# More loads spread over 14 of the 16 DMA engines, earlier field groups, and twelve differences moved to VectorE, in a bilinear pair kernel

## The chip, the cores and the metric

The kernel runs on one core of one Trainium2 chip. The metric is the device time of one execution in microseconds (us). The kernel before has a median of 753.25 us over four runs (753.73, 753.89, 752.77 and 752.07).

## The reference

There are 1024 samples with 32 fields of 128 numbers each, and one 128 x 128 matrix for each of the 496 pairs of fields. For each pair (i, j) the vector of field i is multiplied by the pair's matrix, and the result is multiplied, number by number, by the vector of field j.

```python
v_i = inputs[:, I_IDX, :]          # (1024, 496, 128)
v_j = inputs[:, J_IDX, :]
transformed = jnp.einsum('bpd,ped->bpe', v_i, W)
return transformed * v_j
```

All of it is float32. The output has 1024 x 496 x 128 numbers, 260 MB; the inputs have 49 MB together.

## The kernel before

The host lays the inputs out anew. `xt` holds each field with its 128 numbers down the partitions and the 1024 samples along a row. `wt` holds the matrices in chunks of eight (`WL`), one chunk of 512 KB per load. The pairs are taken with i from 30 down to 0, so that the first pairs need few fields, and the output leaves in groups of four pairs (`OG`), 2 MB each.

**One pair.** A pair is two halves of 512 samples; the loop variable `u` counts halves and `q` counts pairs. After the first 15 pairs, which are multiplied directly (L208), each half is three matrix products into one PSUM bank. The weights and the field are each split into a high part, a low part and a difference: `wh`, `wl`, `wd` (L127 to L130, for two pairs at once) and `xh`, `xl`, `xd` (L142 to L148, per half field). `first(u)` issues two of the products (L211) and lets ScalarE scale the bank (L212). `second(u)`, three halves later, issues the third (L220), and VectorE multiplies the bank by field j into the output tile `ot` (L226). ScalarE's queue issues the store of a finished tile (L257).

**Who splits.** ScalarE makes the high parts. GpSimd makes the low parts and the differences, with one exception: for the first fields that are split (i above 32 - 2 - `NATIVE` - `SHARED`, which is 15) the difference `xd` is put on a list called `later`, and VectorE makes it some halves afterwards (L264). For fields 15 to 0 GpSimd makes it (L148).

**Order.** The order of the program is written out by hand (`tc.manual_schedule()`): each engine and each queue works through its own instructions in the order in which the loop over `u` issues them, and waits where a buffer or an operand is not ready. The weight chunk `c` is loaded at the pair that `w_at` gives it, 17 pairs before its first pair for most of them, into one of three buffers.

**Output buffers.** The tiles of the output rotate over `s0`, `s1`, `s2` and, as long as they are free, over the four buffers `g0` to `g3`. Buffer `g{k}` is later filled with the fields 4k+1 to 4k+4 by one load of 2 MB (`load_group(k)`), at the pair `group_at` names; output tiles leave it alone from 20 pairs (`OWAIT`) before that. So there are seven buffers for output at first, and three from pair 293 on. In the kernel before, `g3`, `g2`, `g1`, `g0` are filled at pairs 79, 141, 219 and 313.

**Which DMA engines a load uses.** SyncE's queue spreads the 128 partitions of a load over 16 DMA engines, eight rows each. Seven of the weight chunks (`WAPART`) are loaded by `load_apart` in two parts instead. GpSimd's queue loads the first 112 partitions with 14 in the outermost place (L102), which makes 14 engines carry eight rows each; SyncE's queue loads the other 16 partitions (L103), one row to each of 16 engines. Some pairs later `move_on` issues a tiny load into a tile called `mark` (L99) that takes the two engines left out, so that the next load of this kind begins at the same engine again. The host puts the rows of these chunks into the order that this needs.

Of the kernel before, what the change touches and what calls it, by code (L numbers as in the profile page):

```python
# [11 lines left out]
P = 128  # L12
NF = 32
NQ = NF * (NF - 1) // 2
BT = 1024
# [3 lines left out]
OG = 4  # L19
EPS = 2.0**-12  # L20
NATIVE = 5
SHARED = 10
XDLAG = 10
LAG = 3
WB = 3
# [4 lines left out]
XG = 4  # L30
NE = 14
ROWS = 8 * NE
WAPART = (45, 47, 49, 51, 54, 58, 60)
BACK = 3
XWAIT = 12
OWAIT = 20
SLAG = 2

# [7 lines left out]
def kernel(  # L46
# [22 lines left out]
    nc = tc.nc  # L69
# [12 lines left out]
    def load_x(f, pieces=1, eng=None):  # L82
        if f == 0:

            t = rpool.tile([P, WL, P], F32, tag="w", name="x_0").rearrange("p q e -> p (q e)")
        else:
            t = xpool.tile([P, BT], F32, tag=f"x{f}", name=f"x_{f}")
        s = BT // pieces
        for k in range(pieces):
            (eng or nc.sync).dma_start(out=t[:, k * s : (k + 1) * s], in_=xt[f, :, k * s : (k + 1) * s])  # L90
        x_sb[f] = t
# [5 lines left out]
    def move_on(k):  # L97

        nc.gpsimd.dma_start(out=mark[: 2 * k], in_=xt[0, : 2 * k, :16].rearrange("(b a) n -> a b n", a=k))  # L99

    def load_apart(dst, src):
        nc.gpsimd.dma_start(out=dst[:ROWS], in_=src[:ROWS].rearrange("(b a) m n -> a b m n", a=NE))  # L102
        nc.sync.dma_start(out=dst[ROWS:], in_=src[ROWS:])  # L103

    def load_group(k):
        t = xpool.tile([P, XG, BT], F32, tag=f"g{k}", name=f"x_g{k}")
        f = XG * k + 1
        nc.sync.dma_start(out=t, in_=xt[f : f + XG].rearrange("m d b -> (m d b)").rearrange("(d m b) -> d m b", m=XG, b=BT))
        for m in range(XG):
            x_sb[f + m] = t[:, m, :]  # L110

    def load_w(c, splits=(0, WL), eng=nc.sync):
        w_raw[c] = rpool.tile([P, WL, P], F32, tag="w", name=f"w_{c}")
        if c in WAPART:
            load_apart(w_raw[c], wt[c])
            return
        for a, b in zip(splits, splits[1:]):
            eng.dma_start(out=w_raw[c][:, a:b, :], in_=wt[c, :, a:b, :])
# [17 lines left out]
    def split_x(f, a, u):  # L136
# [7 lines left out]
        nc.gpsimd.tensor_scalar(l, l.bitcast(F32), 1.0 / EPS, 1.0, ALU.mult, ALU.mult)  # L144
        if f > NF - 2 - NATIVE - SHARED:
            later.append((min(u + XDLAG, 2 * first_q[f] + LAG - 1), d, h.bitcast(F32), l.bitcast(F32)))
# [5 lines left out]
    first_q = {i: q for q, (i, j) in reversed(list(enumerate(pairs)))}  # L152
# [31 lines left out]
    back = []  # L184

    ngroup = NF // XG // 2
    group_at = {first_q[XG * k + XG + 1] - XWAIT: k for k in range(ngroup)}
    until = {f"g{k}": q - OWAIT for q, k in group_at.items()}
    used = {t: n - 9 for n, t in enumerate(("s0", "s1", "s2", *sorted(until, reverse=True)))}

# [10 lines left out]
    def first(u):  # L201
        q, h = divmod(u, 2)
        i, c = pairs[q][0], q // WC
        r = slice(q % WC * P, (q % WC + 1) * P)
        s = slice(h * HB, (h + 1) * HB)
        po[u] = ppool.tile([P, HB], F32, tag="po", name=f"po_{u}")
        if q < nq0:
            nc.tensor.matmul(po[u], w_raw[q // WL][:, q % WL, :], x_sb[i][:, s], start=True, stop=True)  # L208
        else:
            for t in (0, 1):  # L210
                nc.tensor.matmul(po[u], w_s[c][t][:, r], x_s[i][t][:, s], start=t == 0, stop=t == 1)  # L211
            nc.scalar.mul(po[u], po[u], 1.0 + EPS)  # L212

    def second(u):
        q, h = divmod(u, 2)
        i, j = pairs[q]
        r = slice(q % WC * P, (q % WC + 1) * P)
        s = slice(h * HB, (h + 1) * HB)
        if q >= nq0:
            nc.tensor.matmul(  # L220
                po[u], w_s[q // WC][2][:, r], x_s[i][2][:, s], start=False, stop=True, skip_group_check=True
            )
        g, k = divmod(q, OG)
        if k == 0 and h == 0:
            ots[g] = out_tile(g)
        nc.vector.tensor_tensor(ots[g][:, k, s], po.pop(u), x_sb[j][:, s], ALU.mult)  # L226
        if q >= NQ - 2:
            stores.append((u + SLAG, out[g, :, k, s], ots[g][:, k, s]))
        elif g == 0 or q >= NQ - OG:
            if h == 1:  # L230
                stores.append((u + SLAG, out[g, :, k], ots[g][:, k]))
        elif k == OG - 1 and h == 1:
            stores.append((u + SLAG, out[g], ots[g]))

    for u in range(2 * NQ + LAG + SLAG):
        q = u // 2
        if u < 2 * NQ:
            i, j = pairs[q]
            if u % 2 == 0 and j == i + 1 and XG * ngroup < i - 2 - XLEAD:
                load_x(i - 2 - XLEAD)  # L240
            first(u)
            if u == 2 * nq0:
                move_on(5)
            if u % 2 == 0 and q in group_at:
                load_group(group_at[q])
            if u % 2 == 1 and q in w_at:
                load_w(w_at[q])
                if w_at[q] in WAPART:
                    back.append(q + BACK)
            if u % 2 == 0 and q in back:  # L250
                move_on(16 - NE if q < w_q[WAPART[-1]] else 13)
            if u == 2 * x_at + 1:
                load_x(0)
        if LAG <= u < 2 * NQ + LAG:
            second(u - LAG)
        while stores and stores[0][0] <= u - LAG:
            nc.scalar.dma_start(*stores.pop(0)[1:])  # L257
        if u % 2 == 1:
            ready = [t for t in todo if t[0] <= q]
            if ready:  # L260
                ready[0][2](u)
                todo.remove(ready[0])
        while later and later[0][0] <= u:
            nc.vector.tensor_tensor(*later.pop(0)[1:], ALU.subtract)  # L264
# [33 lines left out]
```

## Time and profile before

| | before |
|---|---|
| median of four runs | 753.25 us |
| the profiled execution | 753.73 us |
| its span, first to last instruction | 752.0 us |
| TensorE (PE) busy | 701.1 us, 93% |
| VectorE (DVE) busy | 651.8 us, 87% |
| ScalarE (ACT) busy | 626.9 us, 83% |
| GpSimd (POOL) busy | 602.7 us, 80% |
| moved by DMA | 310.05 MB, 412 GB/s |
| queue q10 (ScalarE's issues: nearly all stores) | 261.10 MB, 82.2% of 16 engines' span |
| queue q1 (SyncE's issues: loads) | 45.03 MB, 15.4% |
| queue q0 (GpSimd's issues) | 3.22 MB, 1.2% |

An engine's busy time is the time in which one of its instructions runs. A DMA queue's share is the time that its packets took, over sixteen engines for the whole span. A queue name with a q at its end (SPq, ACTq, POOLq) is the part of an engine that issues transfers. Times in the profile count from the first instruction.

### The profile page before, as it was taken

The page shows a single profiled execution, that of the slowest core. Times are in us where ns is not written, and L with a number is a line of the kernel's source. Part 1 is how long each engine was busy: PE and PEld are TensorE (multiplying, and loading weights), DVE is VectorE, ACT ScalarE, POOL GpSimd, SP SyncE. Part 2 cuts the span into 40 slices and gives each one's busy share as a digit, 9 for nine tenths or more (in the row PEclk, how much of TensorE's full clock was granted, in tenths as well). Part 3 has the DMA queues.
Part 4 walks back from the last instruction along what each step waited for, and adds up shares of the span by engine and source line. Part 5 has one row for each costly group of instructions (what it writes and reads, how often), then busy time and mean ns, then how long its engine had stood idle before and what let it go on. Part 6 is the DMA issues. An engine that isn't in the chain of part 4 may idle for free.

```text
span 752.0 us, 10964 instructions
## 1 busy us (share of the span) xinstructions
PE 701.1 (93%) x2946; PEld 552.4 (73%) x2946; DVE 651.8 (87%) x1012; ACT 626.9 (83%) x1256; POOL 602.7 (80%) x878
## 2 busy tenths in 40 slices
PE   7998999999999999989999997899999999999993
PEld 3576777777778778767777776678778787777782
DVE  4899999998999999777889877789898989788893
ACT  1298889998889889878898895789999898888892
POOL 1789999999999898886988875878888979797670
PEclk9999999999999999999999998999999999999997
DMA  9999999999999999999999997999999999999997
GB/s 344 422 430 428 410 427 392 423 431 428 430 412 429 430 424 428 424 421 424 414 428 408 418 411 302 374 429 427 417 418 429 413 425 409 427 426 423 420 417 300
DMA packets 31790, 310.05 MB, mean 412 GB/s; under 512 B 3953, under 2 KB 4081, under 8 KB 15601
## 3 DMA queue, kind: packets, MB, share of 16 engines
q10 hardware_dynamic: 19584, 261.10, 82.2%
q1 hardware_dynamic: 10880, 45.03, 15.4%
q0 software_dynamic: 1264, 3.22, 1.2%
q8 instruction: 24, 0.39, 0.2%
q14 instruction: 38, 0.30, 0.1%
HBM read 49.29 MB, written 260.05 MB: 411 GB/s over the span
## 4 chain that ended last, share of the span: by engine, by line
PE 61%; DMA 19%; POOL 9%; DVE 6%; issue 2%; ACT 1%; DVEq 0%; ACTq 0%; POOLq 0%
PE po L211 39%; PE po L220 19%; DMA out_dram<-ot 19%; DVE ot L226 5%; PE po L208 4%; POOL xd L148 3%; POOL wl L128 2%; POOL xl L143 2%; POOL xl L144 1%; POOL wd L130 1%; DMA x<-in_xt_dram 1%; POOL wd L129 1%; DVE xd L264 1%; ACT po L212 0%; ACT wh L127 0%
## 5 line engine op out<-in xcount | busy, mean ns | idle before, releaser
L212 ACT ACTIVATE po<-po 128x512 f32<-128x512 f32 x962 | 545.7, 583 | 92.8 <-PE po L211 49.3
L226 DVE TENSOR_TENSOR ot<-po,x 128x512 f32<-128x512 f32 x720 | 464.1, 685 | 68.2 <-DMA out_dram<-ot 33.9
L211 PE MATMUL po<-xl,wl 128*128 128x512 f32 x962 | 378.8, 394 | 17.7 <-POOL wl L128 16.4
L211 PE MATMUL po<-xh,wh 128*128 128x512 f32 x962 | 379.3, 394 | 14.8 <-DVE ot L226 14.5
L220 PE MATMUL po<-xd,wd 128*128 128x512 f32 x962 | 376.2, 391 | 1.8 <-DVE xd L264 0.9
L128 POOL TENSOR_TENSOR wl<-w,wh 128x256 fp32r<-128x256 f32 x241 | 181.0, 751 | 66.7 <-ACT wh L127 64.4
L211 PEld LDWEIGHTS po<-xh,wh 128*128 128x128 f32 x962 | 181.5, 189 | 62.9 <-DVE ot L226 24.7
L211 PEld LDWEIGHTS po<-xl,wl 128*128 128x128 f32 x962 | 181.4, 189 | 62.7 <-POOL wl L128 24.5
L220 PEld LDWEIGHTS po<-xd,wd 128*128 128x128 f32 x962 | 181.6, 189 | 40.8 <-ACT po L212 2.4
L130 POOL TENSOR_TENSOR wd<-wl,wd 128x256 fp32r<-128x256 f32 x241 | 178.1, 739 | 20.1
L226 DVE TENSOR_TENSOR ot<-po,x_g 128x512 f32<-128x512 f32 x272 | 172.2, 684 | 21.0 <-DMA out_dram<-ot 10.0
L129 POOL TENSOR_SCALAR wd<-wh 128x256 fp32r<-128x256 f32 x241 | 98.6, 409 | 20.4
L127 ACT ACTIVATE wh<-w 128x256 fp32r<-128x256 f32 x241 | 99.3, 412 | 5.2 <-DVE ot L226 5.2
L148 POOL TENSOR_TENSOR xd<-xh,xl 128x512 fp32r<-128x512 f32 x32 | 41.4, 1292 | 2.7
L143 POOL TENSOR_TENSOR xl<-x_g,xh 128x512 fp32r<-128x512 f32 x32 | 41.5, 1296 | 0.2 <-ACT xh L142 0.2
L143 POOL TENSOR_TENSOR xl<-x,xh 128x512 fp32r<-128x512 f32 x20 | 26.3, 1315 | 15.7 <-ACT xh L142 15.4
L144 POOL TENSOR_SCALAR xl<-xl 128x512 fp32r<-128x512 f32 x52 | 34.8, 670 | 4.6
L208 PE MATMUL po<-x,w 128*128 128x512 f32 x60 | 29.0, 644 | 4.1 <-DMA x<-in_xt_dram 4.1
L208 PEld LDWEIGHTS po<-x,w 128*128 128x128 f32 x60 | 11.9, 205 | 20.4 <-issue 12.3
L142 ACT ACTIVATE xh<-x 128x512 fp32r<-128x512 f32 x20 | 12.4, 628 | 11.4 <-DMA x<-in_xt_dram 11.3
L142 ACT ACTIVATE xh<-x_g 128x512 fp32r<-128x512 f32 x32 | 20.2, 631 | 0.0
L264 DVE TENSOR_TENSOR xd<-xh,xl 128x512 fp32r<-128x512 f32 x20 | 19.8, 989 | 0.0
(7 smaller groups left out, 11.2 us busy)
## 6 DMA issues: line engine op xcount, KB each, us to landing
out_dram<-ot ACTq DMA_DIRECT2D x122, 2048.0 KB, 13.9
w<-in_wt_dram SPq DMA_DIRECT2D x54, 512.0 KB, 10.8
x_g<-in_xt_dram SPq DMA_DIRECT2D x4, 2048.0 KB, 18.9
x<-in_xt_dram SPq DMA_DIRECT2D x14, 512.0 KB, 9.5
w<-in_wt_dram POOLq DMA_DIRECT2D x7, 448.0 KB, 12.2
out_dram<-ot ACTq DMA_DIRECT2D x6, 512.0 KB, 9.4
x<-in_xt_dram ACTq DMA_DIRECT2D x4, 256.0 KB, 5.9
out_dram<-ot ACTq DMA_DIRECT2D x4, 256.0 KB, 8.3
```

The source lines that it names most:

```text
L127: nc.scalar.mul(h, raw, 1.0 - 2.0**-13)
L128: nc.gpsimd.tensor_tensor(l, raw, h.bitcast(F32), ALU.subtract)
L129: nc.gpsimd.tensor_scalar(d, h.bitcast(F32), EPS, 1.0, ALU.mult, ALU.mult)
L130: nc.gpsimd.tensor_tensor(d, l.bitcast(F32), d.bitcast(F32), ALU.subtract)
L143: nc.gpsimd.tensor_tensor(l, x_sb[f][:, s], h.bitcast(F32), ALU.subtract)
L144: nc.gpsimd.tensor_scalar(l, l.bitcast(F32), 1.0 / EPS, 1.0, ALU.mult, ALU.mult)
L148: nc.gpsimd.tensor_tensor(d, h.bitcast(F32), l.bitcast(F32), ALU.subtract)
L208: nc.tensor.matmul(po[u], w_raw[q // WL][:, q % WL, :], x_sb[i][:, s], start=True, stop=True)
L211: nc.tensor.matmul(po[u], w_s[c][t][:, r], x_s[i][t][:, s], start=t == 0, stop=t == 1)
L212: nc.scalar.mul(po[u], po[u], 1.0 + EPS)
L220: nc.tensor.matmul(po[u], w_s[q // WC][2][:, r], x_s[i][2][:, s], start=False, stop=True, skip_group_check=True)
L226: nc.vector.tensor_tensor(ots[g][:, k, s], po.pop(u), x_sb[j][:, s], ALU.mult)
```

## The change

Three numbers and the rules around them change.

- `load_group` sends groups 1 and 2 (fields 5 to 8 and 9 to 12) through `load_apart`, as eight more weight chunks now are. These are chunks 20, 26, 30, 32, 36, 38, 40 and 42, all before the seven that were there. Each such load is followed by a `move_on`.
- The groups are loaded at pairs 52, 129, 207 and 313, given in a list; `until`, which says how long a group's buffer serves for output, follows from it.
- `SHARED` goes from 10 to 16, so VectorE also makes the differences of fields 15 to 10, two halves each.

```diff
-SHARED = 10
+SHARED = 16
...
-WAPART = (45, 47, 49, 51, 54, 58, 60)
+WAPART = (20, 26, 30, 32, 36, 38, 40, 42, 45, 47, 49, 51, 54, 58, 60)
 BACK = 3
-XWAIT = 12
+XAT = (313, 207, 129, 52)
+XAPART = (1, 2)
...
-        nc.sync.dma_start(out=t, in_=xt[f : f + XG].rearrange("m d b -> (m d b)").rearrange("(d m b) -> d m b", m=XG, b=BT))
+        rows = xt[f : f + XG].rearrange("m d b -> (m d b)").rearrange("(d m b) -> d m b", m=XG, b=BT)
+        if k in XAPART:
+            load_apart(t, rows)
+        else:
+            nc.sync.dma_start(out=t, in_=rows)
...
-    group_at = {first_q[XG * k + XG + 1] - XWAIT: k for k in range(ngroup)}
+    group_at = {q: k for k, q in enumerate(XAT)}
+    assert all(q < first_q[XG * k + XG + 1] for q, k in group_at.items())
...
                 load_group(group_at[q])
+                if group_at[q] in XAPART:
+                    back.append(q + BACK)
...
-    for f in range(1, XG * 4, XG):
-        xt[f : f + XG] = xt[f : f + XG].transpose(1, 0, 2).copy().reshape(XG, P, BT)
+    for k in range(4):
+        f = XG * k + 1
+        some = xt[f : f + XG].transpose(1, 0, 2).copy()
+        if k in XAPART:
+            some[:ROWS] = some[:ROWS].reshape(NE, 8, XG, BT).transpose(1, 0, 2, 3).reshape(ROWS, XG, BT).copy()
+        xt[f : f + XG] = some.reshape(XG, P, BT)
```

## The prediction

> **What bounds the kernel now.** I read the page's slices first, then busy time by stretch, then the waits in the stretch that stands out, then the packet records of the trace (queue, start, duration and size of every DMA packet).
>
> ```profile
> span 752.0 us, 10964 instructions
> DMA  9999999999999999999999997999999999999997
> GB/s 344 422 430 428 410 427 392 423 431 428 430 412 429 430 424 428 424 421 424 414 428 408 418 411 302 374 429 427 417 418 429 413 425 409 427 426 423 420 417 300
> ```
>
> The DMA engines are busy all the time, while PE has 93%, DVE 87%. So bytes per engine set the time. One place in mid-span is open: slices 25 and 26, about 451 to 489 us, with 302 and 374 GB/s. Busy time by stretch (start:end, length, busy by engine, then granted PE clock, DMA share, GB/s):
>
> ```profile
> core 0: us, PE busy (x) PEld busy (x) DVE busy (x) ACT busy (x) POOL busy (x), PEclk, DMA share, GB/s
> 200.00:330.00 130.00, 123.32 (x536) 100.02 (x537) 117.42 (x176) 115.57 (x234) 114.90 (x166) 1.00 1.01 424
> 330.00:448.00 118.00, 112.62 (x476) 89.16 (x475) 98.03 (x160) 102.43 (x205) 95.43 (x142) 0.99 1.00 417
> 448.00:484.00 36.00, 29.53 (x119) 23.60 (x119) 26.86 (x40) 25.59 (x52) 24.50 (x36) 0.91 0.82 336
> 457.00:459.00 2.00, 2.00 (x6) 1.56 (x5) 1.97 (x4) 1.02 (x2) 0.00 (x0) 0.50 0.19 80
> 484.00:600.00 116.00, 111.59 (x484) 89.97 (x483) 100.49 (x161) 103.56 (x209) 97.95 (x147) 1.00 1.01 422
> ```
>
> At 457 us most DMA engines are empty and PE runs at half its clock. The waits of 440 to 484 us say what came before:
>
> ```profile
> DVE ot L226 <- DMA out_dram<-ot: 7.8, 2, 6.9
> PEld po L211 <- DVE ot L226: 5.8, 1, 5.8
> ```
>
> DVE stood 6.9 us until a store had left its buffer (448 to 454.9 us); PE stood behind it, came back at clock 0.5, and fed the stores too slowly.
>
> Why was that store late when the engines are empty just after? Its sixteen end markers (4-byte packets) tell. It was issued at 437.2 us; eleven engines ended it by 445.2 us, the last one at 454.2. One engine was 9 us behind. The packets say why: from 165 to 310 us, where chains of packets can be followed engine by engine, 16 KB usually lasts 611 ns on fifteen engines and 635 on one, 4 KB 159 against 166. One engine is 4% slow. Its lag behind the middle one grows from nothing at 30 us to 2.9 at 165, near 4 at 205 and 7.7 at 306; a lag of 9 us with three or four buffers is the stall.
>
> Store latency (issue to landing) agrees. The first line is 330 to 448 us, the second 484 to 600, where chunks 45 to 54 already go over 14 engines:
>
> ```profile
> out_dram<-ot ACTq DMA_DIRECT2D x19, 2048.0 KB, 17.6
> out_dram<-ot ACTq DMA_DIRECT2D x21, 2048.0 KB, 11.5
> ```
>
> In that later part the lag stays near 2 us, so the slow engine must be one of the two left out; the packet durations of those loads fit too.
>
> **The change part by part.** The sum is against the profiled run (753.73 us, span 752.0); its median is 0.5 us less.
>
> *Relief of the slow engine.* A chunk load gives it 1 row of 4 KB instead of 8, the other fourteen 9: relative to them 8 x 159 ns = 1.27 us. A group load does it with 16 KB rows: 8 x 611 ns = 4.9 us. The lag grows 3.5 us per 100 us (4.8 in 140). Group 2 at about 204 us takes the 4 us away; from there to 317 us come 4.0, chunks 20, 26 take 2.5; group 1 takes the rest; from 317 to 480 us come 5.7, chunks 30 to 40 take 6.4. So around 450 us the lag should be 0 to 2 us, and the 6.9 us stall has no cause. What is late next is the middle engine, at 8 us after issue against three buffers' 16 us.
>
> *What the hole is worth.* 36 us x (1 - 336/422) = 7.3 us. In 330 to 448 us the slow engine set the pace while the others ran thin: 118 x (1 - 417/424) = 1.9 us. After 484 us the relieving loads are unchanged, so the 3 us by which the slow engine ends last (750.3 against 747.4) remain; I take 0.5 us, between 0 and 3.
>
> *What it costs.* The other fourteen engines carry one more row per load: 2 x 611 + 8 x 159 ns = 2.5 us, in full, since they will set the pace.
>
> *GpSimd.*
>
> ```profile
> L102 POOL DMA_DIRECT2D w<-in_wt_dram x7: 622/622/625, 523.1 to 693.6; - x7
> L99 POOL DMA_DIRECT2D mark<-in_xt_dram x8: 632/633/746, 31.4 to 699.0; - x8
> L148 POOL TENSOR_TENSOR xd<-xh,xl x32: 1263/1296/1304, 170.6 to 663.5; 128x512 fp32r<-128x512 f32 x32
> L264 DVE TENSOR_TENSOR xd<-xh,xl x20: 682/868/1573, 19.1 to 157.7; 128x512 fp32r<-128x512 f32 x20
> ```
>
> Ten loads and ten `mark` issues more: 10 x (0.62 + 0.63) = 12.6 us; twelve differences fewer: 12 x 1.30 = 15.5. Net 3 us less: nothing. A 2 MB issue by GpSimd is in no row; with as many rows as a chunk, 0.62 us is the near value; if each row were cut into four, 2.5 us, once per group. In its queue the weight splits wait behind it, and PE behind those. It must not meet a wait there: group 2's buffer last holds output group 22, landed at 163.6 us in this trace, and GpSimd reaches the load at about 204 (start of chunk 67's split); group 1: group 43, 289.4 against 312. SyncE's 16-row parts wait on the same buffers: no wait.
>
> *VectorE.* Twelve differences at 0.87 to 0.99 us: 10.4 to 11.9 us between about 180 and 330 us. By busy time this fills it: 117.4 of 130 us already. But its operations overlap: six in a row took 3.69 us, 0.615 us each, against PE's 0.45 + 0.23 = 0.68 per half (two L211 and one L220 in the chain). For the 100 pairs from 120 to 219, 200 x 0.615 + 11.9 = 135 us against PE's 136 and the DMA engines' 25 groups x 5.8 = 145 (5.8 us between store issues from 338 to 448 us). Cost 0; without the overlap 200 x 0.685 + 11.9 = 149, 4 us over DMA (bound 0 to 12).
>
> *Earlier groups.* Group 3's buffer is last used by output group 3 (landed 49.5 us), so SyncE can issue the load at about 78 us (now 112.7); weight loads behind it wait only the issue, 0.5 us. Up to 35 us earlier, 5 us of DMA time moves and none is added. Output has six buffers instead of seven for some 45 us, and latency there is 10.5 us against six buffers' 33: 0, between -1 and +1. Groups 2 and 1 were issued at 205.6 and 317.9 and move a few us; each is needed some 30 us later.
>
> Sum: -7.3 - 1.9 - 0.5 + 2.5 = -7.2, so 746.5 for such an execution and 746.0 for a median.
>
> *A rule against it.* All loads on 16 engines in 330 to 448 us left one engine 9 us behind the rest. The Trainium skill, "DMA: Bandwidth & Descriptors", section "Rules for kernel authors", says to use all 16 engines and put a multiple of 16 outermost, which treats them as equal; by it the sum would be +2.5 us alone. The same page ("Latency and other measured facts") calls two engines usually slower and guesses at the software queue's descriptor rings; by that guess ten more GpSimd loads would feed the slowness. This trace speaks against the guess: the 4% was measured where no such load runs.
>
> **The rivals.**
>
> *VectorE becomes the bound (slower).* For it: 97% busy (67.95 of 70 us) from 130 to 200 us. Against it: the 0.615 us pitch. It decides once a half costs VectorE over 0.68 us with the differences in: 200 x 0.685 + 11.9 is 13 us over PE; if the whole 12.7 us reaches the stores, -7.2 + 12.7 = +5.5, about 758.5. Stores in flight (15 to 19 us of latency) would hide most of it. Chance 0.09.
>
> *The hole stays.* Three buffers start at pair 293 and group 0's 2 MB still go over 16 engines by SyncE. If another stall of over 3 us halves the clock there, only 1.9 + 0.5 - 2.5 is left: 753. Chance 0.09.
>
> *The relief does not reach the slow engine* (the 14 engines begin elsewhere): +2.5, 755.5; the flat lag after 484 us speaks against it. Chance 0.03.
>
> *More is gained.* The slow engine's 3 us at the end go too, and 90 to 120 us, where stores were briefly slower, gains 2: 741.5. Chance 0.12.
>
> **How the numbers follow.** The forecast has 0.67, its own range 743 to 750 (hole 5 to 8, tail 0 to 3, group 3 +-1). 740.5 to 751.5 takes in the better case and stops short of the others' values: about 0.2 is left out. Telling it from no change takes 0.2%, 1.5 us. Faster: 0.67 + 0.12 + a third of the hole's 0.09 and a little less for misses, 0.82; same 0.06; slower 0.12.
>
> **What would show it.** Right: no slice under 390 GB/s in mid-span; no half clock near 455 us; store latency from 330 to 448 us down from 17.6 to 12 to 15 us; DVE waits for stores spread out, none over 4 us. Wrong: DVE full from 180 to 330 us with stores landing within 10 us of issue (VectorE's rival); DMA share under 0.95 somewhere new; a GpSimd gap before its 2 MB issues; one engine still 5 us behind at 440 us.

## The result, and the profile after

| | before | after |
|---|---|---|
| median | 752.0 us (56 runs, 749.89 to 756.15) | 750.96 us (35 runs, 748.77 to 755.66) |
| ratio to before | | 0.999, 95% [0.998, 1.0] |
| the profiled execution, its span | 753.73 us, 752.0 us | 750.96 us, 749.1 us |

No change that can be measured, where 0.9% was forecast. The four runs shown before the prediction were, with 753.25 us, 1.25 us above the median of all 56.

The head of the page after, in the rows shown of before:

```profile
span 749.1 us, 11026 instructions
PE 698.6 (93%) x2946; PEld 554.3 (74%) x2946; DVE 664.8 (89%) x1024; ACT 624.9 (83%) x1256; POOL 604.0 (81%) x886
PEclk9999999999999999979999999999999999999997
DMA  9999999999999999999999999999999999999998
GB/s 345 424 428 427 431 424 430 426 430 426 400 388 428 424 426 431 401 372 419 430 414 429 427 405 426 413 406 380 413 382 423 417 425 415 416 431 424 425 432 341
```

The slices of 302 and 374 GB/s are gone. In their place stand four shallower ones, at 388, 372, 380 and 382 (slices 12, 18, 28 and 30, counted from 1). The first two are new places: 206 to 225 and 318 to 337 us, where groups 2 and 1 are loaded (issued at 199.58 and 312.22 us). Note the row DMA: the engines are as busy there as anywhere, they only move less. The same stretches as before, and two more around the group loads:

```profile
core 0: us, PE busy (x) PEld busy (x) DVE busy (x) ACT busy (x) POOL busy (x), PEclk, DMA share, GB/s
330.00:448.00 118.00, 113.89 (x488) 93.11 (x489) 112.75 (x167) 103.88 (x208) 97.70 (x146) 0.98 1.00 420
448.00:484.00 36.00, 31.97 (x139) 25.65 (x138) 28.95 (x45) 30.02 (x61) 31.48 (x47) 1.00 1.01 421
484.00:600.00 116.00, 109.60 (x470) 88.76 (x470) 102.84 (x160) 100.07 (x201) 94.26 (x141) 0.99 0.99 404
203.00:219.00 16.00, 16.00 (x72) 13.27 (x71) 16.00 (x25) 15.31 (x32) 14.63 (x22) 1.00 1.01 368
315.00:331.00 16.00, 8.41 (x37) 6.70 (x36) 6.45 (x11) 8.89 (x19) 14.19 (x19) 0.82 1.01 367
```

The hole of 448 to 484 us is filled: 421 GB/s where it was 336, PE at full clock. But 484 to 600 us fell from 422 to 404, and beside each group load the engines move 368 and 367 GB/s at a share of 1.01. In the second of these PE works only half of the time (8.41 of 16 us), part of it at half clock. The waits of 295 to 345 us (us in all, times, the longest), and then those of 440 to 520 us:

```profile
DVE ot L232 <- DMA out_dram<-ot: 11.0, 3, 8.6
PEld po L217 <- DVE ot L232: 8.6, 3, 8.0
```

```profile
DVE ot L232 <- DMA out_dram<-ot: 11.5, 5, 4.3
```

A stall of the kind that was removed stands in a new place. The store that VectorE waits for until 329.9 us was in flight beside group 1's load, and PE's clock is halved for 10.2 us from 325.2 us on. Two smaller stalls end at 482.7 and 491.7 us, where group 0's 2 MB are loaded and output has three buffers. The issue rows of the page after (KB each, median us to landing):

```profile
x_g<-in_xt_dram SPq DMA_DIRECT2D x2, 2048.0 KB, 20.5
x_g<-in_xt_dram POOLq DMA_DIRECT2D x2, 1792.0 KB, 18.4
```

**Lost DMA time.** To see all stretches at once I added up, from the trace's packet records, what the packets of each stretch take at their usual durations (16 KB 611 ns, 4 KB 159 ns, less 4 ns of overlap each). The stretch less this sum, per engine, is time in which the engines stood or their packets lasted longer. The nominal sum is 722 us in both kernels. The row "all" has the rest of the span too. Columns are us lost; "e2" (the groups back on 16 engines) and "e11" (the same 14 engines, other partitions) are experiments told of below.

| stretch, us | before | before, again | after | e2 | e11 |
|---|---|---|---|---|---|
| 55-130 | 2.8 | 3.7 | 0.3 | 0.3 | 0.3 |
| 180-225 | 0.8 | 0.7 | 3.2 | 0.3 | 1.0 |
| 290-345 | 0.7 | 0.6 | 4.0 | 1.3 | 1.1 |
| 345-448 | 3.4 | 4.2 | 2.3 | 3.9 | 2.3 |
| 448-484 | 8.0 | 6.4 | 0.8 | 1.1 | 1.1 |
| 484-520 | 0.2 | 0.2 | 3.3 | 3.0 | 4.4 |
| 520-740 | 5.1 | 4.1 | 5.6 | 5.7 | 5.3 |
| all | 29.9 | 26.7 | 26.9 | 23.1 | 22.4 |
| span | 752.0 | 748.8 | 749.1 | 745.3 | 744.9 |

The hole gave its 7 us. The two group loads took 5.7 of them back (0.8 + 0.7 became 3.2 + 4.0), and 484 to 520 us took 3.1. A second profile of the kernel after lost 2.3 and 3.5 us at the group loads but only 1.0 in 484 to 520 us: the first price belongs to the kernel, the second differs between executions.

### The profile page after: what moved, and what is told of

Same layout as the page of the kernel before. It is cut to its first block, busy times and chain, and to the rows that moved or that the text cites. A ratio compares the mean times of both kernels' runs of the same rounds, so it can differ in the third digit from the quotient of the medians.

```text
span 749.1 us, 11026 instructions
## 1 busy us (share of the span) xinstructions
PE 698.6 (93%) x2946; PEld 554.3 (74%) x2946; DVE 664.8 (89%) x1024; ACT 624.9 (83%) x1256; POOL 604.0 (81%) x886
## 3 DMA queue, kind: packets, MB, share of 16 engines
q10 hardware_dynamic: 19584, 261.10, 82.7%
## 4 chain that ended last, share of the span: by engine, by line
PE 61%; DMA 18%; POOL 9%; DVE 8%; issue 2%; ACT 1%; DVEq 0%; ACTq 0%; POOLq 0%
PE po L217 40%; PE po L226 19%; DMA out_dram<-ot 17%; DVE ot L232 7%; POOL wl L133 3%; PE po L214 2%; POOL xl L148 2%; POOL xd L153 2%; POOL wd L135 1%; DVE xd L272 1%; POOL xl L149 1%; POOL wd L134 1%; DMA x<-in_xt_dram 1%; ACT po L218 1%; ACT wh L132 0%
## 5 line engine op out<-in xcount | busy, mean ns | idle before, releaser
L133 POOL TENSOR_TENSOR wl<-w,wh 128x256 fp32r<-128x256 f32 x241 | 183.1, 760 | 64.6 <-ACT wh L132 58.9
L226 PEld LDWEIGHTS po<-xd,wd 128*128 128x128 f32 x962 | 182.0, 189 | 41.1 <-ACT po L218 2.4
L232 DVE TENSOR_TENSOR ot<-po,x_g 128x512 f32<-128x512 f32 x272 | 174.8, 685 | 33.6 <-DMA out_dram<-ot 21.5
L272 DVE TENSOR_TENSOR xd<-xh,xl 128x512 fp32r<-128x512 f32 x32 | 30.2, 943 | 0.0
L153 POOL TENSOR_TENSOR xd<-xh,xl 128x512 fp32r<-128x512 f32 x20 | 25.8, 1290 | 1.7
```

The lines of the kernel that those rows point to most:

```text
L133: nc.gpsimd.tensor_tensor(l, raw, h.bitcast(F32), ALU.subtract)
L153: nc.gpsimd.tensor_tensor(d, h.bitcast(F32), l.bitcast(F32), ALU.subtract)
L226: nc.tensor.matmul(po[u], w_s[q // WC][2][:, r], x_s[i][2][:, s], start=False, stop=True, skip_group_check=True)
```

## The experiments

Each is told with its ratio to runs of the kernel before on the same chip; the 95% intervals reach some 0.2 to 0.3% to each side, and gains in us are worked out from the ratio. Where an edit is shown for a variant of the kernel after, it is shown against that kernel.

**The kernel before, once more** (one execution):

> The kernel before, unchanged, for a second profile of it. If the stall near 450 us with the half clock belongs to the kernel, it is there again, with 7 us of DMA time lost (stretch 448 to 484 us under 350 GB/s) and one store end marker 9 us behind the others just before it. If it was a mishap of one execution, the stretch has over 410 GB/s and the span is 3 to 7 us shorter; then the gain forecast for the change was largely counted against a mishap.

750.6 us, and the hole is there again. Stretch 448 to 484 us of that run:

```profile
448.00:484.00 36.00, 30.56 (x128) 24.51 (x127) 26.82 (x42) 27.19 (x56) 25.87 (x38) 0.95 0.87 354
```

The stall belongs to the kernel (6.2 us at 455.3 us), but it cost 1.6 us less than in the execution that the sum was made against.

**Only the weight chunks**, on the kernel before:

```diff
-WAPART = (45, 47, 49, 51, 54, 58, 60)
+WAPART = (20, 26, 30, 32, 36, 38, 40, 42, 45, 47, 49, 51, 54, 58, 60)
```

> The kernel before with only the eight more weight chunks over 14 engines; groups over 16 engines at their old pairs, ten fields' differences on VectorE. Relief theory (the slow engine's lag is what costs, and the group loads from GpSimd give the gain back): lag of the slow engine at 440 us about 3 to 5 us instead of 9, the stall near 450 us gone or under 4 us, 2 to 5 us faster than before. GpSimd theory (the ten more issues slow GpSimd, which VectorE's twelve differences are there to pay for): PE waits for GpSimd's weight parts rise by 5 us or more, and the time is within 1 us of before.

747.6 us, 0.9939 [0.9917, 0.9961]: 4.6 us faster than before. The same stretch:

```profile
448.00:484.00 36.00, 31.96 (x131) 25.61 (x132) 30.00 (x46) 28.21 (x57) 28.49 (x42) 0.95 0.96 392
```

The hole is half filled, with a stall of 3.9 us left at 449 us. One line of the change does more than the whole, as the first theory said (2 to 5 us).

**The groups back on 16 engines**, all else as in the kernel after:

```diff
-XAPART = (1, 2)
+XAPART = ()
```

> The changed kernel, but groups 1 and 2 go over 16 engines by SyncE's queue as before, still at pairs 207 and 129. Relief theory with a price at the group loads: the DMA time lost around the two loads (180 to 220 and 300 to 340 us) falls from about 3.2 and 3.8 us to 1 each, the 8.6 us stall of VectorE near 325 us shrinks to under 4, and the kernel is 2 to 5 us faster than the changed one, 3 to 6 faster than before. If instead the relief by the groups is needed, the slow engine's lag reaches 8 us or more again before 450 us, and the time is that of before or worse. VectorE theory: no difference from the changed kernel, since its twelve differences are still there.

747.01 us, 0.9921 [0.9898, 0.9944]: 5.9 us faster than before. The stretches around the group loads in this kernel:

```profile
203.00:219.00 16.00, 16.00 (x71) 13.00 (x70) 13.62 (x23) 15.28 (x32) 13.93 (x21) 1.00 1.01 428
315.00:331.00 16.00, 15.46 (x68) 12.43 (x67) 13.71 (x23) 14.45 (x30) 12.06 (x19) 1.00 1.01 428
484.00:600.00 116.00, 111.44 (x479) 90.47 (x478) 104.20 (x160) 102.44 (x206) 97.33 (x145) 0.99 0.99 404
```

428 GB/s beside the same 2 MB. So sending the groups over 14 engines in this form is what costs, by time and by place; the loss after 484 us is another matter, since it stays. VectorE's stall of 8.6 us goes too: its longest wait from 295 to 345 us is 2.9 us.

**GpSimd's twelve differences back**, on the kernel after:

```diff
-SHARED = 16
+SHARED = 10
```

> The changed kernel, but GpSimd makes the differences of fields 15 to 10 again, as before. VectorE theory (it was 70.00 of 70 us busy from 130 to 200 us after the change, and that is where the gain went): 2 to 4 us faster than the changed kernel. DMA theory (the engines set the time, VectorE has room): within 1 us of the changed kernel; DMA time lost at the group loads the same. GpSimd theory: PE waits for GpSimd's weight parts between 180 and 330 us rise by 3 us or more, and the kernel is up to 2 us slower than the changed one.

751.73 us, 0.9988 [0.9972, 1.0004]. The twelve differences neither cost nor gain.

**The other two engines left out**, on the kernel with the weight chunks alone; the tiny load moves the place where the next load begins by four engines more:

```diff
-                move_on(5)
+                move_on(9)
...
-                move_on(16 - NE if q < w_q[WAPART[-1]] else 13)
+                move_on(16 - NE if q < w_q[WAPART[-1]] else 9)
```

> The version with the eight more weight chunks alone, but the first small load covers nine engines instead of five, so that all fifteen chunk loads leave out another two engines. Relief theory: the slow engine now carries nine rows of each such load instead of one and falls behind faster than in the kernel before (whose seven loads relieved it); its lag passes 9 us, stalls of VectorE for stores return in the second half too, and the time is 5 to 15 us over that version (747.6), at or above the kernel before. Rival (which engines are left out does not matter, the gain comes from GpSimd's queue as a second way for loads): within 1 us of 747.6.

759.27 us, 1.0093 [1.0076, 1.011]: 12 us over the same kernel with the right two engines left out. Its stretch and its wait there:

```profile
448.00:484.00 36.00, 28.50 (x117) 22.76 (x116) 25.86 (x40) 24.97 (x51) 24.31 (x36) 0.91 0.85 338
```

```profile
DVE ot L226 <- DMA out_dram<-ot: 7.5, 1, 7.5
```

The same loads, the same bytes, the same issues; only which engines carry less is different. That one slow engine sets the pace, and that the relief reaches it, is shown.

**Why are the group loads slow?** Their 16 KB packets last 726 to 756 ns on average in two profiles of the kernel after, not 611. Weight packets beside them take 205 to 223 ns instead of 159, and stores 665 to 705 instead of 611. Candidates: GpSimd's queue, the size of the burst, the order in which the rows are read, the order in which they are written. First GpSimd's queue over all 16 engines:

```diff
-            load_apart(t, rows)
+            nc.gpsimd.dma_start(out=t, in_=rows)
...
```

> The changed kernel, but groups 1 and 2 are loaded by GpSimd's queue over all 16 engines, eight rows of 16 KB each in the ordinary order, with no part by SyncE. It tells GpSimd's queue from the 14-engine form. If the price of the group loads comes from a third queue that shares the engines with the two others (the 2 MB runs beside a weight load instead of behind it): packets stretched as in the changed kernel (16 KB of the group at over 700 ns), about 2 to 3 us lost at each of the two loads, time as the changed kernel within 1.5 us. If it comes from the 14-engine form (its row order or its longer share per engine): packets at 611 to 620 ns as with SyncE's queue, loss under 1 us each, 3 to 4 us faster than the changed kernel.

749.45 us, 0.9951 [0.9927, 0.9975]; packets of 645 ns. The stretches:

```profile
203.00:219.00 16.00, 16.00 (x72) 13.24 (x71) 15.28 (x24) 15.31 (x33) 14.52 (x22) 1.00 1.01 423
315.00:331.00 16.00, 14.67 (x65) 11.60 (x63) 11.28 (x18) 13.89 (x29) 13.65 (x19) 1.00 1.01 410
```

So it is not the queue; it is the form that spreads a group over 14. (The profiled execution, 745.1 us, is the fastest of seven; the gain of 3.7 us is not told apart from the 5.9 of SyncE's loads by these intervals.)

**The groups apart, field by field**, 448 KB at a time at pairs 129, 133, 137, 149 and 207, 211, 215, 227:

```diff
+XFIELD = {1: (207, 211, 215, 227), 2: (129, 133, 137, 149)}
...
+            load_apart(t[:, m : m + 1, :], rows[:, m : m + 1, :])
```

> The changed kernel, but groups 1 and 2 go over 14 engines field by field: four loads of 448 KB by GpSimd, some pairs apart, with 4 KB packets, as the weight chunks have them. If the length of the burst is what costs: lost DMA time around the groups (180 to 220, 300 to 345 us) falls from 3.2 and 3.8 us to under 1.5 each, and the kernel is 3 to 5 us faster than the changed one, near the version with the groups on 16 engines. If any byte by this route costs the same: no change within 1.5 us, or slower by the six more loads and marks on GpSimd (7.5 us of its time).

749.02 us, 0.9955 [0.9938, 0.9972]: 3.4 us faster than before. The stretches:

```profile
203.00:219.00 16.00, 13.75 (x55) 10.89 (x55) 12.29 (x19) 12.16 (x26) 11.10 (x19) 0.91 1.01 422
315.00:331.00 16.00, 14.05 (x63) 11.30 (x61) 14.12 (x22) 14.01 (x29) 14.06 (x20) 1.00 1.01 423
```

At its place the price is gone: 336 packets of 4 KB by GpSimd's queue between 204 and 227 us last 159 ns on average, and 180 to 225 and 290 to 345 us lose 0.4 and 0.6 us. So eight neighbouring partitions on 14 engines do not cost this by themselves; it takes the 16 KB rows, all in one load, as well. By the ratio the kernel gains 2.5 us less than with the groups on 16 engines; the intervals overlap, and the profiled executions, which lose some 23 us in all in both, do not show where that would be lost.

**The memory rows in natural order.** The kernel after reads rows that the host has put 16 KB x 14 in turn; here each engine reads its own 8 rows in a run, from an input of its own:

```diff
-            load_apart(t, rows)
+            nc.gpsimd.dma_start(out=t[:ROWS], in_=xg[k - 1, :, :8])
+            nc.sync.dma_start(out=t[ROWS:], in_=rows[ROWS:])
...
```

> The changed kernel, but the rows of groups 1 and 2 that go over 14 engines lie in memory in their natural order, eight rows of one engine in a run (an input of its own, with a gap of one row behind each run, so that 14 stays the outermost place), instead of fourteen engines' rows side by side. Memory-order theory (fourteen engines that read neighbouring 16 KB rows at the same time get in each other's way): packets of the group loads fall from about 756 ns to under 660, the loss at each load to under 1.5 us, and the kernel is 3 to 5 us faster than the changed one. Rival (14 engines with nine rows each beside weight loads and stores are slow whatever the order): packets stay over 720 ns, time within 1.5 us of the changed kernel.

751.31 us, 0.9986 [0.9966, 1.0006]; packets of 760 ns. The order of reading falls. On the same chip the kernel after itself:

> The changed kernel, unchanged, beside the next three on the same chip. Within 1 us of the kernel before, as in its first measurement (ratio 0.999). Its profile shows again 16 KB packets of the group loads at over 700 ns and 2 to 4 us of lost DMA time at each of the two loads, if these belong to it.

752.33 us, 0.9992 [0.997, 1.0014]; packets of 726 ns, and 2.3 and 3.5 us lost at the two loads.

**Three quarters of the stores away.** This shows what the loads take by themselves, and what computing takes:

```diff
-            stores.append((u + SLAG, out[g], ots[g]))
+            stores.append((u + SLAG, out[g, :, :1], ots[g][:, :1]))
```

On the kernel before:

> The kernel before, with only the first of each group's four pairs stored (the last group whole): three quarters of the output are left out, all computing stays. It measures how long the computing alone takes. If computing has much room (the forecast took 145 us of DMA time against 136 of PE for 100 pairs), about 690 to 705 us. If computing is a second bound close behind the DMA engines, 725 to 745 us; then no relief of DMA engines could have brought the forecast's 7 us.

729.46 us, 0.9702 [0.9671, 0.9732]: computing is close behind the DMA engines. The conclusion that the expectation draws from this, that no relief could have brought 7 us, does not hold: versions below gain up to 6.7. On the kernel after:

> The changed kernel, with three quarters of the output left out in the same way. VectorE's twelve differences and GpSimd's ten more issues and marks show by its distance from the last: within 2 us if the move from GpSimd to VectorE is even; 5 us or more over it if VectorE becomes the bound, as the slower rival of the forecast had it.

721.01 us, 0.9581 [0.9556, 0.9606]. Neither of the two cases: it is 8.4 us under the last. Two things follow. Computing is 8.4 us shorter in the kernel after; what PE waits for GpSimd's low parts falls with it (the kernel before with a quarter of the stores, then the kernel after):

```profile
PE po L211 <- POOL wl L128: 22.0, 21, 1.8
```

```profile
PE po L217 <- POOL wl L133: 15.1, 15, 1.8
```

So VectorE, with its twelve differences, bounds nothing. And the group loads, with little traffic beside them, are slower still. The stretches at the two group loads:

```profile
201.00:212.00 11.00, 11.00 (x51) 9.09 (x50) 11.00 (x18) 10.41 (x22) 10.21 (x16) 1.00 0.91 204
305.00:316.00 11.00, 11.00 (x50) 9.09 (x50) 11.00 (x17) 10.68 (x23) 10.07 (x15) 1.00 0.93 220
```

The engines are 91 and 93% busy and move 204 and 220 GB/s; the packets last 1178 and 1161 ns. The 2 MB loads by SyncE over 16 engines in the same run have 707 and 657, so even beside these it is some 1.7 times as long. Fourteen group packets are in flight at a time, one for each engine. The issue rows of this kernel put the two forms of group load side by side:

```profile
x_g<-in_xt_dram SPq DMA_DIRECT2D x2, 2048.0 KB, 9.4
x_g<-in_xt_dram POOLq DMA_DIRECT2D x2, 1792.0 KB, 13.5
```

Fewer bytes in more time. With the stores running the stretches at the two loads show 368 and 367 GB/s; that the stores' packets fill part of what is lost fits this, and is not shown by itself. The stores are not needed for the slowness: what hinders these loads is among themselves.

**The same 14 engines, other partitions.** With 14 outermost, by the order in which the load names its rows, each engine writes eight neighbouring partitions. Here the 112 rows go in six loads of 12, 32 and 12 partitions, twice, so that an engine writes four neighbours and four more 32 partitions further on. The length of the rows, the engines left out and the queue stay (SyncE's 16 rows go in two loads of eight).

```diff
+    def load_ports(dst, src):
+        for h in (0, 32):
+            for p, n, a in ((20 + h, 12, 3), (64 + h, 32, 8), (h, 12, 3)):
+                nc.gpsimd.dma_start(out=dst[p : p + n], in_=src[p : p + n].rearrange("(b a) m n -> a b m n", a=a))
+            if h == 0:
+                nc.gpsimd.dma_start(out=mark2, in_=xt[0, :4, :16].rearrange("(b a) n -> a b n", a=2))
+            nc.sync.dma_start(out=dst[12 + h : 20 + h], in_=src[12 + h : 20 + h])
...
-            load_apart(t, rows)
+            load_ports(t, rows)
...
```

> The changed kernel, but groups 1 and 2 go to the same fourteen engines in six loads each (12, 32 and 12 partitions, twice), so that an engine writes two runs of four neighbouring partitions, 32 apart, instead of one run of eight. Port theory: in the run of the changed kernel with few stores the group packets of 16 KB took 1178 and 1161 ns instead of 611, nearly twice, with almost nothing beside them; so the engines wait for each other on the side of the destination, in step, and only with this layout. Then the group packets fall from 726 to 756 ns to under 660, the traffic during a group load rises from 355 to 382 GB/s to over 405, the lost time at each load falls under 1.5 us, and the kernel is 3 to 6 us faster than the changed one (relief of the groups kept, their price gone): 745 to 749 us. Rival (fourteen engines with 16 KB rows from GpSimd's queue are slow in any layout): packets over 700 ns, time within 1.5 us of the changed kernel, or 1 to 3 us slower by the twelve more issues (7.5 us of GpSimd's time). The Trainium skill (DMA: Bandwidth & Descriptors, The descriptor swizzle) gives the partitions that one engine writes in an ordinary load as two such runs of four, all behind one port of SBUF; the layout tried here is that one.

**746.35 us, 0.9911 [0.989, 0.9933]**: 6.7 us faster than before. Packets last 615 ns. The stretches:

```profile
203.00:219.00 16.00, 14.68 (x58) 12.01 (x59) 12.71 (x20) 12.16 (x25) 14.78 (x23) 0.89 1.01 427
315.00:331.00 16.00, 15.65 (x68) 12.39 (x66) 13.62 (x24) 15.01 (x31) 14.95 (x22) 1.00 1.01 420
```

So 14 engines as such do not cost it. Six issues in place of one are changed along with the layout, and they thin the load out: a group's packets take 23 us instead of 13, so fewer are in flight at a time. The packet records answer this rival. Where five to nine other packets of the group are in flight, they last 619 ns on average here (92 packets), against 766 and 742 in the two profiles of the kernel after (172 each). So it is not the thinning; the partitions that an engine writes remain. A run with six loads and the old layout would have parted the two fully, and there is none. In time, 0.9911 is not told apart from the 0.9921 of the groups on 16 engines: the mended layout takes the price away, and what the groups add to the relief is not seen. The Trainium skill, "DMA: Bandwidth & Descriptors", section "The descriptor swizzle", says that in an ordinary load of 128 partitions one engine's eight partitions are two runs of four, 32 apart, behind one port of the on-chip memory. The run agrees with the page in that this form has 615 ns where eight neighbours have 726 to 756. That engines which walk through neighbours in step meet at the same few ports is my explanation, and no run shows it: the runs show that the layout matters.

**What is left after 484 us.** Group 0 in four loads of 512 KB by SyncE, at pairs 313, 330, 356 and 384, on the kernel with the groups on 16 engines:

```diff
-XAPART = (1, 2)
+XAPART = ()
+XFIELD = {0: (313, 330, 356, 384)}
...
+            nc.sync.dma_start(out=t[:, m : m + 1, :], in_=rows[:, m : m + 1, :])
```

> The version with groups 1 and 2 over 16 engines, with group 0 loaded field by field (4 loads of 512 KB by SyncE at pairs 313, 330, 356, 384) instead of 2 MB at once. Theory of the moved hole (three output buffers cannot bridge a 2 MB load, so VectorE stalls twice for about 4 us near 480 to 490 us, PE's clock halves, and the DMA engines run thin from 500 to 560 us): no VectorE wait over 3 us there, stretch 484 to 600 us back from 404 to over 418 GB/s, 2 to 4 us faster than the version with 2 MB (747.0 in the last call). Rival, that the thin stretch belongs to the old 14-engine chunk loads: no change within 1 us.

745.48 us, 0.9911 [0.9888, 0.9934]. The stalls at 480 to 490 us are gone (the longest wait for a store from 470 to 500 us is 1.9 us) and 484 to 600 us has 411 GB/s for 404, not the 418 expected:

```profile
484.00:600.00 116.00, 110.05 (x467) 86.67 (x468) 95.86 (x158) 100.03 (x200) 96.34 (x144) 1.00 1.01 411
```

Against the groups on 16 engines alone (0.9921) the gain of some 0.8 us is inside both intervals, and short of the 2 to 4 us expected.

**More relief.** Eight more chunks over 14 engines (12, 14, 16, 18, 22, 24, 28 and 34), with the groups on 16:

```diff
-WAPART = (20, 26, 30, 32, 36, 38, 40, 42, 45, 47, 49, 51, 54, 58, 60)
+WAPART = (12, 14, 16, 18, 20, 22, 24, 26, 28, 30, 32, 34, 36, 38, 40, 42, 45, 47, 49, 51, 54, 58, 60)
...
-XAPART = (1, 2)
+XAPART = ()
```

> The version with the groups on 16 engines, and 23 instead of 15 weight chunks over 14 engines (all even ones from 12 to 42 now). Relief theory: the slow engine loses 4% of 722 us, 29 us, and 23 chunks of 1.27 us give that back without the groups; its lag stays under 4 us up to 340 us instead of 8 to 9, VectorE's waits near 293 to 316 us shrink from 5.3 us to under 3, and it is 1 to 3 us faster than with 15 chunks (747.0). GpSimd theory (eight more loads and marks, 10 us of its time): PE waits for GpSimd rise by 4 us or more and nothing is gained, or 1 to 2 us lost.

748.85 us, 0.9958 [0.9936, 0.998]: at the store that ends near 332 us the last engine is only some 2 us behind the middle one, but VectorE's longest wait from 280 to 340 us is 4.5 us instead of 5.3, and nothing is gained over 15 chunks. The same with group 0 field by field:

> As the last, and group 0 field by field. If the 2 MB of group 0 against three output buffers costs something by itself, 1 to 3 us faster than the last, without VectorE waits over 3 us near 480 to 490 us; otherwise the same within 1 us.

748.01 us, 0.9941 [0.9921, 0.9962]. A miss as well: a second dose of relief brings nothing.

**Lighter computing.** The third product and its operands are left out, so that DMA sets the time nearly alone:

```diff
-        nc.gpsimd.tensor_scalar(d, h.bitcast(F32), EPS, 1.0, ALU.mult, ALU.mult)
-        nc.gpsimd.tensor_tensor(d, l.bitcast(F32), d.bitcast(F32), ALU.subtract)
...
-        if f > NF - 2 - NATIVE - SHARED:
-            later.append((min(u + XDLAG, 2 * first_q[f] + LAG - 1), d, h.bitcast(F32), l.bitcast(F32)))
-        else:
-            nc.gpsimd.tensor_tensor(d, h.bitcast(F32), l.bitcast(F32), ALU.subtract)
...
-        if q >= nq0:
-            nc.tensor.matmul(
-                po[u], w_s[q // WC][2][:, r], x_s[i][2][:, s], start=False, stop=True, skip_group_check=True
-            )
```

On the kernel before, on the kernel after, and on the one with the groups on 16 engines:

> The kernel before without the third product and without the two difference parts (wd, xd): the output is less exact, all loads and stores stay. It measures the DMA engines alone: stores are ready early. If the slow engine alone sets the time of the kernel before, 744 to 750 us; if the mean engine does, 735 to 740.

> The changed kernel without the third product and the difference parts. If the spread over 14 engines does for the DMA engines what the forecast said (no slow engine, 2.5 us more on the others), 8 to 12 us under the last. If the group loads give it back inside the DMA engines (stretched packets, 4 to 6 us), 3 to 6 us under the last. If relief is worth nothing, equal.

> The version with the groups on 16 engines, without the third product and the difference parts, like the two light runs before (745.7 for the kernel before, 751.3 for the changed one): the DMA engines alone. If the group loads over 14 engines are what made the changed kernel's DMA work longer, this one is under the light kernel before: 738 to 744 us. If the chunk loads cost as well, or the earlier group pairs do, 746 to 751.

745.7 us (0.9913 [0.9887, 0.9939]), 751.25 us (0.9983 [0.9967, 0.9998]) and 745.35 us (0.9897 [0.9874, 0.992]). The kernel after gains nothing from having a third less to multiply: its transfers set its 751 us, 5.5 us more than those of before. With the groups back on 16 engines these 5.5 us go. That settles where the change's gain went. It also shows a limit (745.35 lies between the two cases of its expectation): with the relief and 16-engine groups the light kernel is no faster than the light kernel before. Its 448 to 484 us are 5 us better (1.4 us lost for 6.6), and 520 to 740 us are 4 us worse (9.0 for 5.0).

## Why the prediction was wrong, step by step

**The step that failed** is "What it costs": one more row per load, "2 x 611 + 8 x 159 ns = 2.5 us, in full". It counted rows and took each at the duration that rows had on 16 engines, without a range. On 14 engines, eight neighbouring partitions to each, a group's rows of 16 KB last 726 to 756 ns each, and what lies beside them is stretched too. Measured as lost DMA time this is 2.4 + 3.3 = 5.7 us on top of the 2.5 (4.3 in the second profile); measured by the two edits that undo it, 5 to 6 us (0.9921 and 0.9911 against 0.999). With 8.2 us for the term the sum becomes -9.7 + 8.2 = -1.5 us; measured were -0.75 us (the ratio) and -1.0 us (the medians). That these agree so well is in part luck: two changes that the sum did not have, +3.1 us in 484 to 520 us and some -3 us in 55 to 130 us, nearly cancel in this profile.

No row of the page of before has this price. Queue q0, which carried nothing but the seven chunks on 14 engines and the tiny loads, moved 3.22 MB in 1.2% of 16 engines' span: 0.012 x 16 x 752.0 / 3.22 = 45 us per MB, where ScalarE's q10 took 0.822 x 16 x 752.0 / 261.10 = 37.9 and SyncE's q1 41.1. That looks like a warning, but packet by packet most of it goes: the 4 KB packets of q0 last 174 ns on average and those of q1 168, with 159 in the middle of both. A load of 16 KB rows over 14 engines was in no run, and 611 ns came from another form of load.

**The base.** The sum stood against the profiled run of 753.73 us and went to a median half a microsecond less. The median over 56 runs is 752.0, so 1.25 us of the forecast's distance is the base and not the change. The hole was also deep in the run that I had (8.0 us lost, 6.4 in the next). The gain itself, once the layout is mended, is 6.7 us (0.9911 of 753.41) against 7.2 forecast; it too has the 3 us in 55 to 130 us that the sum did not have, and 4.4 us lost in 484 to 520 us, where the kernel before lost 0.2.

**Relief of the slow engine: right in kind, too large in size.** At the store issued near 440 us the last engine is 3.6 us behind the middle one, where it was 9 and 0 to 2 was forecast. That was enough for the stall to go. Left out in the wrong place, the same loads cost 12 us.

**What the hole is worth: right, and its successor missed.** "What is late next is the middle engine, at 8 us after issue against three buffers' 16 us" overlooked the load of group 0, 2 MB between stores that have three buffers: stalls of 4.3 and 4.1 us, 3.1 us more lost in 484 to 520 us (in the second profile none over 3.0 us there). That is also the rival "the hole stays" in part: not there, but 35 us later and half as deep, at full clock but for 3.4 us. Of the 330 to 448 us term (1.9 us), 345 to 448 us shows 1.1 us of lost time. The tail's 0.5 us cannot be told from the scatter.

**GpSimd: right.** Its 2 MB issues took 0.62 us each with no wait before them:

```profile
L103 POOL DMA_DIRECT2D x_g<-in_xt_dram x2 | 1.2, 624 | 0.0
```

**VectorE: right.** It is busier (70.00 of 70 us from 130 to 200 us, 89% over all), and neither giving its differences back nor taking the stores away shows a price.

**The earlier group 3: too small.** 0 was put, between -1 and +1. 55 to 130 us lost 2.8 and 3.7 us in the two profiles of before and 0.3 in after. That the earlier load is the cause is not shown by a run of its own: the kernel with only the weight chunks, which loads it late, lost 1.7, and differs from the one with the groups on 16 engines, which loads it early, by 0.6 us in the medians.

**The signs.** "No slice under 390 GB/s", "no wait over 4 us" were wrong, at the places above. "No half clock near 455 us" and "store latency down to 12 to 15 us" (13.9) came true; they speak of the hole alone, and not of what was paid for it. The listed signs of failure did not hold the one that came: DMA share at 1.01 with less moved. A full engine that is slow looks like a full engine.

**The rule weighed.** The Trainium skill, "DMA: Bandwidth & Descriptors", section "Rules for kernel authors", wants all 16 engines and a multiple of 16 outermost. For the weight chunks the runs are against it (0.9939 with 14); for the groups they are with it (0.9921 with 16 against 0.999 with 14) until the partitions are laid out otherwise (0.9911 with 14, no worse than 16). The guess on the software queue's rings on the same page finds no support here: from 165 to 310 us, where one engine was measured as 4% slow, the kernel before has no packet on that queue.

**What stays open.** Why 520 to 740 us loses 4.1 to 9.4 us, by an amount that differs between executions (5.6 and 7.6 in two of the kernel after) and is largest with group 0 field by field (9.4), with 23 chunks (9.0) and in the last light kernel (9.0); what is gained before comes back there in part. Whether the weight chunks, whose packets of 4 KB last 172 to 188 ns on average on 14 engines against 165 to 170 by SyncE, gain from the layout of the groups, and whether that layout and group 0 field by field add up: neither was tried. Two versions beat both kernels at 0.9911, the one with the partitions laid out by runs of four and the one with group 0 field by field; nothing here tells them apart, nor from the groups on 16 engines at 0.9921.

## What to carry to other kernels

A balance of bytes over DMA engines is not a balance of time: before moving a load to another set of engines, look which partitions each engine will write, and take the price of a packet from loads of the very same form, length of row and layout included. Where no run has that form, the price needs a range, or a run of its own. Take the competing traffic away to see whether a slow load is slow by itself. And where an effect is 1%, one profiled execution can lie 1.7 us off the median by chance (over 4 us with the groups by GpSimd over 16 engines and with group 0 field by field), so a hole's depth in it is a sample, not a constant.

## What the runs showed of the hardware

- A load over 14 engines with eight neighbouring partitions to each moved 16 KB packets in 1161 and 1178 ns with few stores beside it (ordinary loads in that run: 657 and 707), 726 to 756 with all of them; with two runs of four partitions, 32 apart, 615. Stores beside the first form took 665 to 705 ns for 611. Field by field, in 4 KB packets, the first form had 159 ns at its place and no loss.
- One DMA engine of sixteen is 4% slow (635 for 611 ns), and which two engines fifteen loads of 512 KB leave out is worth 12 us (747.6 against 759.27).
- After a stall of PE its half clock lasted 3.41, 6.83 or 10.24 us in these profiles, always a multiple of 3.41, and the stretches at full clock between were multiples too (27.31 and 157.01 us in the kernel after). The Trainium skill, "TensorE: Matmul & The Clock Gate", Part 1, gives a free-running window of 3413 ns for this; the traces agree.
